# Gathered weights replaced by copies from a resident table in a two-layer conditional SSM kernel

## The chip, the cores and the metric

The kernel runs on one core of one Trainium2 chip. The metric is the device time of one execution in microseconds (us), from which smaller is better. Before the change the median of three runs is 1152.68 us (1152.45 to 1154.42). A "profile" here is one execution recorded by the hardware profiler; its engines are PE (TensorE matmul), PEld (TensorE weight load), DVE (VectorE), ACT (ScalarE), POOL (GpSimd) and SP (SyncE), the last of which only issues transfers.

## The reference

Two residual layers on `x` of shape (64 batches, 128 channels, 2048 steps), all float32.

```python
# layer 0: a batch chooses one of 16 weights of 128 x 128
W = weights[condition]                         # condition: 64 integers in 0..15
x = x + einsum('bct,bcd->bdt', x, W)
# layer 1: a diagonal state space model, 128 channels with 64 states each
K = 2 * einsum('hn,hnl->hl', Ct, exp(dtA * l)).real       # the kernel K(h, l) from log_dt, C, A
y = causal_convolution(x, K) + x * D[:, None]
x = x + y * (arange(2048) < length[batch])     # beyond a batch's length nothing is added
```

## The kernel before, in words

The sequence of 2048 is cut into two segments of 1024 (`SEGS`), and the work falls into two stages.

**Stage A, first segment of layer 0 and the tables of layer 1.** A loop over 64 batches calls `batch0(b)`. `fetch` brings two batches (1 MB) from HBM through SP's queue, nine pairs ahead (`AHEAD`). `weigh` brings the batch's weight with an indirect transfer on POOL's queue (L441), seven batches ahead (`WAHEAD`): the row numbers stand in the tile `rowid`, computed once by DVE. `add_one` (L449) adds the identity to it on DVE, four batches ahead (`ADD`), so that one matmul gives x + xW. `project` runs two matmuls of 128x512 (L457) into a PSUM tile of tag `y` (two buffers), ACT copies the result back over `xb` (L459), and ACT's queue writes it to the scratch `scr` in HBM (L462), from where stage B reads it in another layout.

Beside the batches runs the making of the tables. The setup (`_Parameters`, L116 on) computes rates, frequencies and gains on DVE in small instructions and lays them out by PE transposes (`lay`). From batch 12 on, every batch lets DVE take six steps of the generator `tables()`: for each of the 16 groups g (`NT`) `angles(g)` has 14 steps (L599 to L614) and `products(g)` two (L627, L629). `later(lag, step, g)` puts a group's other work so many batches on: `sines` on ACT (L623, L624) two batches after the angles, and, counted from the products, `lags` on PE one batch on (L641, eight small matmuls that give K), `keep_lags` on ACT two on (L645), `gain_lags` on DVE four on (L651), `store_lags` on POOL's queue six on (L655). `exps` on ACT (L487) come in fours of groups.

Each engine runs its instructions in the order in which this program writes them (the schedule is manual), so a waiting instruction holds everything behind it on its engine. In stage A PE's order is therefore batch, batch, eight `lags` matmuls, batch, and so on.

**Stage B, 64 iterations.** Each iteration handles four channels of one segment: `load` from `scr`, `turn` (PE transposes, L772), `inputs` (L797), `scan` over eight chunks on DVE (L812, L821), `inside` (L838), `outputs` (L850), then `copy_predicated` (L859), which puts the result over `xs` where `mask` is set, and `store`. While the first segment's 32 iterations run, `some(n)` works off the 128 projections ("pieces") of the second segment between the other matmuls; `fetches`, `weights_for` and `add_ones` bring their data, weights and identities ahead of them, by the iteration (`due`). POOL's queue also carries the Toeplitz tiles (L740), a memset (L782) and the carried states (L829).

Memory: the weight tiles `w1` have nine buffers (pool `s0`); the constants `ptab` (eight rows of parameters), `wk`, `drow`, `quarter`, `steps` and the integer `mask` lie in a pool that stays for the whole kernel.

Of the kernel before, what the change touches and what calls it, by code (L numbers as in the profile page):

```python
# [39 lines left out]
F32 = mybir.dt.float32  # L40
I32 = mybir.dt.int32
AF = mybir.ActivationFunctionType
ALU = mybir.AluOpType
# [3 lines left out]
P = 128  # L47
# [10 lines left out]

DRE, FHI, FLO, PHI, AMP, NAMPX, LR, LI = range(8)
NPAR = 8  # L60
Q = 128
SEGS = (1024, 1024)
TP = 4
# [49 lines left out]
class _Parameters:  # L113


    def __init__(self, nc, pool, psp, ptab, wk, ident, log_dt, c_in, log_a_real, a_imag):  # L116
        self.nc, self.V, self.psp, self.ptab, self.wk, self.ident = nc, nc.vector, psp, ptab, wk, ident
        N = self.N = a_imag.shape[1]
# [241 lines left out]

    def row(self, r0):
        return lambda lanes, f, n: self.ptab[lanes, r0 : r0 + n, :].rearrange("p k (j d) -> p k j d", d=2)

# [5 lines left out]
def cond_resid_ssm_kernel(  # L369
# [32 lines left out]
    assert C == P == Q and B == P // 2 and N == P // 2 and TP * Q == BK  # L402

    const = ctx.enter_context(tc.tile_pool(name="const", bufs=1))
    tab = ctx.enter_context(tc.tile_pool(name="tab", bufs=1))
    big = ctx.enter_context(tc.tile_pool(name="big", bufs=10))
    s0 = ctx.enter_context(tc.tile_pool(name="s0", bufs=9))
    dram = ctx.enter_context(tc.tile_pool(name="dram", bufs=1, space=DRAM))
# [6 lines left out]

    rowid = const.tile([P, B], I32, tag="rowid", name="rowid")
    ident = const.tile([P, P], F32, tag="ident", name="ident")
    ptab = const.tile([P, NPAR, NP], F32, tag="ptab", name="ptab")
    wk = const.tile([P, 2, NP, 2], F32, tag="wk", name="wk")
    drow = const.tile([2, NP], F32, tag="drow", name="drow")  # L420
    quarter = const.tile([P, 1], F32, tag="quarter", name="quarter")
    steps = const.tile([P, NE], F32, tag="steps", name="steps")
    mask = const.tile([P, NS, HL], I32, tag="mask", name="mask")

# [3 lines left out]
    AHEAD = 9  # L428
    WAHEAD = 7
    w_rows = weights.rearrange("s c d -> (s c) d")  # L430

# [6 lines left out]
    def weigh(s, b):  # L438

        w1s[s, b] = s0.tile([P, C], F32, tag="w1", name=f"w1_{s}_{b}")  # L440
        nc.gpsimd.indirect_dma_start(  # L441
            out=w1s[s, b],
            out_offset=None,
            in_=w_rows,
            in_offset=bass.IndirectOffsetOnAxis(ap=rowid[:, b : b + 1], axis=0),
        )

    def add_one(s, b):
        nc.vector.tensor_tensor(w1s[s, b], w1s[s, b], ident, ALU.add)  # L449

# [15 lines left out]

    ADD = 4
# [13 lines left out]
    def par_of(row, g, i):  # L481
        return ptab[:, row, g * TP + i : g * TP + i + 1]

    def exps(g):

        for i in range(TP):
            nc.scalar.activation(es[g][:, i, 0, :], steps, AF.Exp, scale=par_of(DRE, g, i))  # L487

    with tc.tile_pool(name="setup", bufs=1) as setup:
        ci = setup.tile([P, B], I32, tag="ci", name="ci")  # L490
        nc.sync.dma_start(ci, cond.rearrange("(o b) -> o b", o=1).to_broadcast([P, B]))
        par = _Parameters(nc, setup, psp, ptab, wk, ident, log_dt, c_in, log_a_real, a_imag)
        chi = setup.tile([P, 1], I32, tag="chi", name="chi")
        chf = setup.tile([P, 1], F32, tag="chf", name="chf")
        nc.gpsimd.iota(chi, [[0, 1]], base=0, channel_multiplier=1)
        make_identity(nc, ident)
# [3 lines left out]

        cf = setup.tile([P, B], F32, tag="cf", name="cf")
        ck = setup.tile([P, B], F32, tag="ck", name="ck")
        V.tensor_copy(chf, chi)
# [4 lines left out]
        V.tensor_copy(cf, ci)  # L508
# [3 lines left out]
        V.tensor_scalar(cf, cf, float(C), chf, ALU.mult, ALU.add)  # L512
        V.tensor_copy(rowid, cf)
        for b in range(WAHEAD):
# [42 lines left out]
        others = _weave(par.decays(), par.decay_of_chunk(), par.inverse())  # L557
        for b in range(ADD):
            run(_weave(freq, others), 8)
            add_one(0, b)  # L560
        run(freq)
# [6 lines left out]
        batch0(3)  # L568
        par.lay("ppar_1", rows, 3, par.row(DRE))
        run(par.gains())  # L570
# [8 lines left out]
        par.phase_sines()  # L579
        par.lay("ppar_2", rows, 1, par.row(PHI))  # L580
# [4 lines left out]
        par.lay("ppar_3", rows, 4, par.row(AMP), swapped=1)  # L585
        rows = par.spread("rows4", (par.wr, 1.0), (par.wi, 1.0))
# [39 lines left out]
    def products(g):  # L626
        V.tensor_tensor(es[g][:, :, 1, :], ts[g][:, 0], es[g][:, :, 0, :], ALU.mult)  # L627
        yield
        V.tensor_tensor(es[g][:, :, 0, :], ts[g][:, 1], es[g][:, :, 0, :], ALU.mult)  # L629
# [29 lines left out]
    FILL = 12  # L659
    begun = told = added = done = 0  # L660

# [23 lines left out]
    def add_ones(n):  # L685
        nonlocal added
        while added < min(n, len(pieces)):
            add_one(*pieces[added][:2])
            added += QB

# [28 lines left out]
    tmp.__exit__(None, None, None)  # L719


# [150 lines left out]
    def iteration(i):  # L872
# [6 lines left out]
        fetches(due(i + 1))  # L879
        weights_for(due(i + 2))  # L880
        if nxt:
# [17 lines left out]
        if nxt:  # L899
            inputs(i + 1, CG - 1)  # L900
            keep_weights(i + 1)
            add_ones(due(i + 1))
            scan(i + 1, 0, 2 if seg(i + 1)[0] == 0 else 1)
# [5 lines left out]
        if nxt:  # L909
            scan(i + 1, 3 if seg(i + 1)[0] == 0 else 2, NQ)  # L910
    add_ones(FILL)
    load(0)
# [37 lines left out]
```

## Time and profile before

| what | value |
|---|---|
| median of 3 runs | 1152.68 us |
| the profiled execution's own time | 1151.87 us |
| its span, first to last instruction | 1150.1 us |
| time outside the span | 1.77 us |
| mean granted TensorE clock | 0.991 of full |
| stage A (to the last projection of the first segment) | 0 to about 206 us |
| PE / DVE / ACT / POOL busy over the span | 94% / 75% / 60% / 26% |

The busy shares are means over two unlike stages and say little by themselves. What a change in a stage is worth is read from that stage: which engine works without a gap there, who waits for whom, and which chain of work ended last. An instruction's duration includes the overlap with the one before it; the time that it takes of its engine is better read from the starts of its neighbours.

### The profile page before, as it was taken

Reading aid. Unit: us, or ns where it says so; the run is one execution under the profiler, and the core shown is the slowest. Engines: PE = TensorE matmul, PEld = TensorE weight load, DVE = VectorE, ACT = ScalarE, POOL = GpSimd, SP = SyncE. Lnnn points to the kernel's source line nnn. Section 1 sums busy time; section 2 is a strip of 40 time slices with the busy share of each in tenths; the row PEclk is TensorE's granted clock in tenths of the full one; section 3 lists DMA queues with packets and bytes.
Section 4 is the critical chain, followed back from the end, with each engine's and each line's share of the span. In section 5 each row is a group of like instructions: output and inputs, shape, how many; then the busy total and the mean of one; then the engine's idle time right before and its main releaser. Section 6 shows DMA issues by size and latency. Waiting matters only on the chain.

```text
span 1150.1 us, 23651 instructions
## 1 busy us (share of the span) xinstructions
PE 1081.0 (94%) x8586; PEld 792.1 (69%) x8586; DVE 867.6 (75%) x2940; ACT 694.0 (60%) x1117; POOL 296.6 (26%) x377
## 2 busy tenths in 40 slices
PE   4587889799999999999999999999999999999996
PEld 2233344367767777777777777888888888888885
DVE  7498895076667667766766677889899899889896
ACT  2557875566666566566656666656656656656551
POOL 5233444322331332233223211221111111111110
PEclk9899999999999999999999999999999999999998
DMA  8999999989999999999999978788887787788854
GB/s 324 411 399 352 386 355 336 365 288 312 308 329 297 310 299 293 317 309 293 298 308 299 291 227 231 228 237 228 216 238 226 217 242 222 212 242 222 212 162 110
DMA packets 120501, 320.62 MB, mean 279 GB/s; under 512 B 13602, under 2 KB 13858, under 8 KB 112194
## 3 DMA queue, kind: packets, MB, share of 16 engines
q1 hardware_dynamic: 70800, 218.16, 61.7%
q10 hardware_dynamic: 35762, 67.32, 15.8%
q0 software_dynamic: 13824, 33.65, 10.6%
q8 instruction: 68, 1.11, 0.4%
q14 instruction: 47, 0.39, 0.1%
HBM read 172.13 MB, written 146.93 MB: 277 GB/s over the span
## 4 chain that ended last, share of the span: by engine, by line
PE 81%; DVE 6%; ACT 5%; DMA 5%; issue 1%; ACTq 1%; SPq 0%; DVEq 0%
PE y L850 21%; PE y L838 19%; PE v L797 18%; PE p L457 11%; PE tr L772 10%; DMA xb<-in_x_dram 2%; PE pb L754 2%; ACT xb L459 1%; DMA scr<-xb 1%; ACT e L487 1%; PE pk L641 1%; DMA x<-scr 1%; DVE t L606 1%; DMA aim<-in_L_cond_A_imag_dram 1%; DVE s L812 1%
## 5 line engine op out<-in xcount | busy, mean ns | idle before, releaser
L812 DVE SCALAR_TENSOR_TENSOR s<-s,ptab 128x128 f32<-128x128 f32 x1792 | 525.7, 355 | 83.3 <-ACT s L802 77.3
L802 ACT ACTIVATE s<-v,ptab 64x512 f32<-64x512 f32 (+1 forms) x512 | 336.7, 658 | 49.8 <-PE v L797 34.2
L838 PEld LDWEIGHTS y<-tt,u 128*128 128x128 f32 x2048 | 263.5, 192 | 80.6 <-issue 67.0
L457 PE MATMUL p<-xb,w 128*128 128x512 f32 x512 | 254.2, 612 | 35.8 <-ACT xb L459 20.7
L838 PE MATMUL y<-tt,u 128*128 128x128 f32 x2048 | 269.9, 275 | 0.2 <-DVE x L859 0.2
L850 PEld LDWEIGHTS y<-e,s 64*128 64x128 f32 x4096 | 233.9, 188 | 46.5 <-issue 24.2
L797 PE MATMUL v<-u,bt 128*128 128x512 f32 (+1 forms) x512 | 248.4, 567 | 0.0
L850 PE MATMUL y<-e,s 64*128 64x128 f32 x4096 | 246.7, 275 | 1.4 <-DVE s L812 1.4
L773 ACT COPY u<-tr 128x512 f32<-128x512 f32 x256 | 150.8, 589 | 157.9 <-PE tr L772 132.3
L821 DVE TENSOR_SCALAR s<-s 128x128 f32<-128x128 f32 x448 | 106.6, 238 | 136.8 <-ACT s L802 136.8
L459 ACT COPY xb<-p 128x512 f32<-128x512 f32 (+1 forms) x192 | 139.3, 726 | 110.8 <-PE p L457 94.3
L859 DVE COPY_PREDICATED x<-mask,y 128x1024 f32<-128x1024 int32 x128 | 171.2, 1338 | 1.1 <-PE y L850 1.0
L441 POOL DMA_INDIRECT w<-in_L_cond_weights_dram,rowid x128 | 131.3, 1026 | 120.0 <-PE p L457 70.5
L457 PEld LDWEIGHTS p<-xb,w 128*128 128x128 f32 x512 | 87.3, 195 | 108.6 <-issue 47.6
L772 PE MATMUL tr<-ident,x 128*128 128x128 f32 x1024 | 156.3, 275 | 5.5 <-DMA x<-scr 5.5
L772 PEld LDWEIGHTS tr<-ident,x 128*128 128x128 f32 x1024 | 121.8, 142 | 56.5 <-issue 51.0
L829 POOL DMA_DIRECT2D carry<-s x64 | 45.1, 755 | 256.5 <-DVE w L449 215.1
L740 POOL DMA_DIRECT2D tt<-kpad x64 | 51.3, 802 | 182.2 <-DVE s L812 171.4
L797 PEld LDWEIGHTS v<-u,bt 128*128 128x128 f32 x512 | 79.6, 191 | 13.9 <-issue 13.6
L785 POOL DMA_DIRECT2D s<-carry x64 | 45.0, 708 | 130.5 <-PE y L850 119.1
L755 ACT COPY bt<-pb 128x512 f32<-128x512 f32 x32 | 18.8, 587 | 87.2 <-PE pb L754 86.6
L782 POOL MEMSET s<- 128x384 f32 x32 | 13.6, 424 | 117.6 <-DMA carry<-s 46.7
(171 smaller groups left out, 357.3 us busy)
## 6 DMA issues: line engine op xcount, KB each, us to landing
xb<-in_x_dram SPq DMA_DIRECT2D x64, 1024.0 KB, 10.9
scr<-xb ACTq DMA_DIRECT2D x128, 512.0 KB, 8.4
x<-scr SPq DMA_DIRECT2D x64, 1024.0 KB, 8.4
out_dram<-x SPq DMA_DIRECT2D x128, 512.0 KB, 5.9
tt<-kpad POOLq DMA_DIRECT2D x64, 256.0 KB, 6.5
btd<-bt SPq DMA_DIRECT2D x32, 256.0 KB, 8.3
bt<-btd SPq DMA_DIRECT2D x32, 256.0 KB, 4.9
carry<-s POOLq DMA_DIRECT2D x64, 64.0 KB, 7.6
```

Source lines behind the costliest of these rows:

```text
L441: nc.gpsimd.indirect_dma_start(out=w1s[s, b], out_offset=None, in_=w_rows, in_offset=bass.IndirectOffsetOnAxis(ap=rowid[:, b : b + 1], axi ...
L457: nc.tensor.matmul(ps[:, k], w1s[s, b], own[:, cols], start=True, stop=True)
L459: nc.scalar.copy(own[:, cols], ps.rearrange("p k t -> p (k t)"))
L772: nc.tensor.transpose(tr[:, k, :], xs[i][:, c, k * Q : (k + 1) * Q], ident)
L773: nc.scalar.copy(u, tr)
L797: nc.tensor.matmul(v[:, 0:nv], w, us[i, n].rearrange("p k r -> p (k r)")[:, 0:nv], start=True, stop=True)
L802: nc.scalar.activation(own[:, 0:nv], v[lanes, 0:nv], AF.Copy, scale=amp)
L812: nc.vector.scalar_tensor_tensor(new[:, d, 0:2], src, factor, own[:, d, 0:2], ALU.mult, ALU.add)
L821: nc.vector.tensor_scalar(old[:, :, 2], old[:, :, 0], -1.0, None, ALU.mult)
L838: nc.tensor.matmul(y[:, k, :], u[:, k, :], tts[i][:, n, :], start=(k == 0), stop=False, skip_group_check=True)
L850: nc.tensor.matmul(ys[i, d][:, c, k, :], st[half[c], d, part, k, :, :].rearrange("p f b -> p (f b)"), e[half[c], pair % TP, part, 0:Q], st ...
L859: nc.vector.copy_predicated(xs[i][:, d::2, :].rearrange("r c (k t) -> r c k t", k=KK), keep_k.unsqueeze(1).to_broadcast([P, 2, KK, Q]), ys ...
```

## The change

The 16 weights (1 MB) are brought once into the tile `wres` by one plain transfer, the first on SP's queue, and DVE adds the identity to all 16 in one instruction of 128x2048 elements. A batch's weight is then copied by POOL from `wres` into a `w1` tile: POOL loads the batch's condition from SBUF into a register and uses it as the offset of the copy. The indirect transfers, `rowid`, and the per-batch `add_one` go. `w1` has four buffers instead of nine and `weigh` runs three batches ahead; for the second segment it is called from `some`, piece by piece, instead of once per iteration.

The matmuls for K and what follows them move two batches on: `lags`, `keep_lags`, `gain_lags`, `store_lags` stand 3, 4, 6 and 8 batches after the products (before: 1, 2, 4, 6), and the loop has two more rounds.

The mask is stored in bytes instead of 32-bit integers. The tables needed only in stage A (`gtab`, the first four rows of the former `ptab`, and `wk`, `drow`, `quarter`, `steps`) move to a pool `early` that is released before stage B. The conditions are read as one row by ACT's queue, ahead of the parameters.

```diff
-    s0 = ctx.enter_context(tc.tile_pool(name="s0", bufs=9))
+    s0 = ctx.enter_context(tc.tile_pool(name="s0", bufs=4))
-    rowid = const.tile([P, B], I32, tag="rowid", name="rowid")
+    ci = const.tile([1, B], I32, tag="ci", name="ci")
+    wres = const.tile([P, S, C], F32, tag="wres", name="wres")
-    mask = const.tile([P, NS, HL], I32, tag="mask", name="mask")
+    mask = const.tile([P, NS, HL], I8, tag="mask", name="mask")
-    WAHEAD = 7
+    WAHEAD = 3
     def weigh(s, b):
         w1s[s, b] = s0.tile([P, C], F32, tag="w1", name=f"w1_{s}_{b}")
-        nc.gpsimd.indirect_dma_start(out=w1s[s, b], out_offset=None, in_=w_rows,
-            in_offset=bass.IndirectOffsetOnAxis(ap=rowid[:, b : b + 1], axis=0))
-    def add_one(s, b):
-        nc.vector.tensor_tensor(w1s[s, b], w1s[s, b], ident, ALU.add)
+        at = nc.values_load(ci[:, b : b + 1], engines=(mybir.EngineType.Pool,), min_val=0, max_val=S - 1, ...)
+        nc.gpsimd.tensor_copy(w1s[s, b], wres[:, bass.ds(at, 1), :].rearrange("p s d -> p (s d)"))
     def batch0(b):
...
-        if b + ADD < B:
-            add_one(0, b + ADD)
...
-        nc.sync.dma_start(ci, cond.rearrange("(o b) -> o b", o=1).to_broadcast([P, B]))
+        nc.scalar.dma_start(craw, cond.rearrange("(o b) -> o b", o=1))
+        nc.sync.dma_start(wres, weights.rearrange("s c d -> c s d"))
...
-        V.tensor_copy(rowid, cf)
+        V.tensor_copy(ci, cf)
+        V.tensor_tensor(wres, wres, ident.unsqueeze(1).to_broadcast([P, S, C]), ALU.add)
...
-        for lag, step in ((1, lags), (2, keep_lags), (4, gain_lags), (6, store_lags)):
+        for lag, step in ((3, lags), (4, keep_lags), (6, gain_lags), (8, store_lags)):
...
         for s, b, q in pieces[done : done + n]:
+            weights_for(done + WAHEAD * QB + 1)
             project(s, b, q, ...)
-    def add_ones(n): ...                      # and its calls
-            weights_for(FILL)                 # at batch 60
-        weights_for(due(i + 2))               # in iteration(i)
-    for now in range(12, B + 7):
+    for now in range(12, B + 9):
     tmp.__exit__(None, None, None)
+    early.__exit__(None, None, None)
```

More of the change, by code (lines that the diff above doesn't have):

```diff
@@ L56 @@
 LOG2E = 1.0 / math.log(2.0)
-DRE, FHI, FLO, PHI, AMP, NAMPX, LR, LI = range(8)
-NPAR = 8
+DRE, FHI, FLO, PHI = range(4)
+AMP, NAMPX, LR, LI = range(4)
+NPAR = 4
 Q = 128
@@ L113, with __init__ @@
 class _Parameters:
-    def __init__(self, nc, pool, psp, ptab, wk, ident, log_dt, c_in, log_a_real, a_imag):
-        self.nc, self.V, self.psp, self.ptab, self.wk, self.ident = nc, nc.vector, psp, ptab, wk, ident
+    def __init__(self, nc, pool, psp, wk, ident, log_dt, c_in, log_a_real, a_imag):
+        self.nc, self.V, self.psp, self.wk, self.ident = nc, nc.vector, psp, wk, ident
         N = self.N = a_imag.shape[1]
@@ L359, in lay, with row @@
                 self.V.tensor_copy(to(lanes, f, n)[:, swapped], got[:, 1 - f, swapped])
-    def row(self, r0):
-        return lambda lanes, f, n: self.ptab[lanes, r0 : r0 + n, :].rearrange("p k (j d) -> p k j d", d=2)
+    def row(self, table, r0):
+        return lambda lanes, f, n: table[lanes, r0 : r0 + n, :].rearrange("p k (j d) -> p k j d", d=2)
     def weight(self, lanes, f, n):
@@ L402, in cond_resid_ssm_kernel @@
     assert C == P == Q and B == P // 2 and N == P // 2 and TP * Q == BK
+    I8 = mybir.dt.uint8
     const = ctx.enter_context(tc.tile_pool(name="const", bufs=1))
@@ L414, in cond_resid_ssm_kernel @@
     carry = dram.tile([NP, P, 2, B], F32, tag="carry", name="carry")
-    rowid = const.tile([P, B], I32, tag="rowid", name="rowid")
+    ci = const.tile([1, B], I32, tag="ci", name="ci")
+    wres = const.tile([P, S, C], F32, tag="wres", name="wres")
     ident = const.tile([P, P], F32, tag="ident", name="ident")
     ptab = const.tile([P, NPAR, NP], F32, tag="ptab", name="ptab")
[L419 to L422, printed above, removed]
-    mask = const.tile([P, NS, HL], I32, tag="mask", name="mask")
+    mask = const.tile([P, NS, HL], I8, tag="mask", name="mask")
     xbs, w1s = {}, {}
@@ L428, in cond_resid_ssm_kernel @@
     AHEAD = 9
-    WAHEAD = 7
-    w_rows = weights.rearrange("s c d -> (s c) d")
+    WAHEAD = 3
     def fetch(s, n):
@@ L440, in weigh @@
         w1s[s, b] = s0.tile([P, C], F32, tag="w1", name=f"w1_{s}_{b}")
[L441 to L445, printed above, removed]
-        )
-    def add_one(s, b):
-        nc.vector.tensor_tensor(w1s[s, b], w1s[s, b], ident, ALU.add)
+        at = nc.values_load(
+            ci[:, b : b + 1],
+            engines=(mybir.EngineType.Pool,),
+            min_val=0,
+            max_val=S - 1,
+            skip_runtime_bounds_check_because="it is clamped above",
+        )
+        nc.gpsimd.tensor_copy(w1s[s, b], wres[:, bass.ds(at, 1), :].rearrange("p s d -> p (s d)"))
     def project(s, b, q, ps, n_banks=1):
@@ L465, in project @@
                 del xbs[s, n]
-    ADD = 4
     def batch0(b):
@@ L481, in par_of @@
     def par_of(row, g, i):
-        return ptab[:, row, g * TP + i : g * TP + i + 1]
+        return gtab[:, row, g * TP + i : g * TP + i + 1]
     def exps(g):
@@ L487, in exps @@
             nc.scalar.activation(es[g][:, i, 0, :], steps, AF.Exp, scale=par_of(DRE, g, i))
-    with tc.tile_pool(name="setup", bufs=1) as setup:
-        ci = setup.tile([P, B], I32, tag="ci", name="ci")
-        nc.sync.dma_start(ci, cond.rearrange("(o b) -> o b", o=1).to_broadcast([P, B]))
[L492 to L495, printed above, removed]
+    early = tc.tile_pool(name="early", bufs=1)
+    earlies = early.__enter__()
+    gtab = earlies.tile([P, NPAR, NP], F32, tag="gtab", name="gtab")
+    wk = earlies.tile([P, 2, NP, 2], F32, tag="wk", name="wk")
+    drow = earlies.tile([2, NP], F32, tag="drow", name="drow")
+    quarter = earlies.tile([P, 1], F32, tag="quarter", name="quarter")
+    steps = earlies.tile([P, NE], F32, tag="steps", name="steps")
+    with tc.tile_pool(name="setup", bufs=1) as setup:
+        craw = setup.tile([1, B], I32, tag="craw", name="craw")
+        nc.scalar.dma_start(craw, cond.rearrange("(o b) -> o b", o=1))
+        nc.sync.dma_start(wres, weights.rearrange("s c d -> c s d"))
+        par = _Parameters(nc, setup, psp, wk, ident, log_dt, c_in, log_a_real, a_imag)
         make_identity(nc, ident)
@@ L498, in cond_resid_ssm_kernel @@
             fetch(0, n)
-        cf = setup.tile([P, B], F32, tag="cf", name="cf")
-        ck = setup.tile([P, B], F32, tag="ck", name="ck")
-        V.tensor_copy(chf, chi)
+        cf = setup.tile([1, B], F32, tag="cf", name="cf")
+        ck = setup.tile([1, B], F32, tag="ck", name="ck")
         V.memset(quarter, math.pi / 2)
@@ L507, in cond_resid_ssm_kernel @@
         V.memset(zero, 0.0)
-        V.tensor_copy(cf, ci)
+        V.tensor_copy(cf, craw)
         V.tensor_scalar(ck, cf, 0.0, float(S), ALU.is_lt, ALU.mult)
@@ L511, in cond_resid_ssm_kernel @@
         V.tensor_scalar(cf, cf, 0.0, float(S - 1), ALU.max, ALU.min)
-        V.tensor_scalar(cf, cf, float(C), chf, ALU.mult, ALU.add)
-        V.tensor_copy(rowid, cf)
+        V.tensor_copy(ci, cf)
+        V.tensor_tensor(wres, wres, ident.unsqueeze(1).to_broadcast([P, S, C]), ALU.add)
         for b in range(WAHEAD):
@@ L557, in cond_resid_ssm_kernel @@
         others = _weave(par.decays(), par.decay_of_chunk(), par.inverse())
-        for b in range(ADD):
-            run(_weave(freq, others), 8)
-            add_one(0, b)
+        run(_weave(freq, others), 32)
         run(freq)
@@ L568, in cond_resid_ssm_kernel @@
         batch0(3)
-        par.lay("ppar_1", rows, 3, par.row(DRE))
+        par.lay("ppar_1", rows, 3, par.row(gtab, DRE))
         run(par.gains())
@@ L579, in cond_resid_ssm_kernel @@
         par.phase_sines()
-        par.lay("ppar_2", rows, 1, par.row(PHI))
+        par.lay("ppar_2", rows, 1, par.row(gtab, PHI))
         run(par.sizes())
@@ L584, in cond_resid_ssm_kernel @@
         batch0(11)
-        par.lay("ppar_3", rows, 4, par.row(AMP), swapped=1)
+        par.lay("ppar_3", rows, 4, par.row(ptab, AMP), swapped=1)
         rows = par.spread("rows4", (par.wr, 1.0), (par.wi, 1.0))
@@ L659, in cond_resid_ssm_kernel @@
     FILL = 12
-    begun = told = added = done = 0
+    begun = told = done = 0
     def due(i):
@@ L683, in weights_for @@
             told += QB
[L685 to L689, printed above, removed]
     plan = {}
@@ L901, in iteration @@
             keep_weights(i + 1)
-            add_ones(due(i + 1))
             scan(i + 1, 0, 2 if seg(i + 1)[0] == 0 else 1)
@@ L910, in iteration @@
             scan(i + 1, 3 if seg(i + 1)[0] == 0 else 2, NQ)
-    add_ones(FILL)
     load(0)
```

## The prediction

> **What bounds the kernel now.** I read the page's slices first (one bound or several?), then busy time by stretch, then who idles in stage A and for whom, then one handover in order of time.
>
> ```profile
> span 1150.1 us, 23651 instructions
> ...
> PE   4587889799999999999999999999999999999996
> ...
> DVE  7498895076667667766766677889899899889896
> ...
> DMA  8999999989999999999999978788887787788854
> ...
> PE 81%; DVE 6%; ACT 5%; DMA 5%; issue 1%; ACTq 1%; SPq 0%; DVEq 0%
> ```
>
> In the view of stretches the columns are length, then busy time (count) of PE, PEld, DVE, ACT and POOL, granted clock, DMA share, GB/s:
>
> ```profile
> 56.60:183.80 127.20, 104.31 (x379) 47.09 (x378) 114.83 (x307) 89.07 (x140) 53.04 (x55) 0.99 1.01 375
> 183.80:206.00 22.20, 22.16 (x86) 10.95 (x87) 5.93 (x20) 11.23 (x14) 10.32 (x13) 1.00 0.85 311
> 231.60:700.00 468.40, 467.50 (x3709) 342.95 (x3708) 321.32 (x1100) 295.52 (x483) 126.29 (x164) 1.00 0.95 298
> 700.00:1127.00 427.00, 427.00 (x4150) 359.82 (x4150) 377.40 (x1287) 260.27 (x422) 77.16 (x108) 1.00 0.79 220
> ```
>
> From 231.6 to 1127 us PE works without a gap and the chain lies on it; DVE, ACT and POOL have room. What the change does there is worth nothing unless it makes PE wait. All that can move is in the first 206 us, mostly in the 127.2 us (43 batches, 2.96 each) where tables and batches run together and no engine is full. The waits of DVE, PE and ACT in that stretch (total us, times, longest):
>
> ```profile
> DVE krow L651 <- ACT krow L645: 8.6, 6, 2.5
> ...
> PE p L457 <- ACT xb L459: 11.2, 12, 1.8
> PE pk L641 <- DVE e L629: 9.9, 10, 1.9
> ...
> ACT xb L459 <- PE p L457: 20.9, 11, 6.3
> ```
>
> the row of the adds in the same stretch (busy us, mean ns, idle before):
>
> ```profile
> L449 DVE TENSOR_TENSOR w<-w,ident 128x128 f32<-128x128 f32 x43 | 12.2, 285 | 0.0
> ```
>
> and one handover:
>
> ```profile
> 83.08 0.70 DVE L629 TENSOR_TENSOR e<-t,e 128x516 f32<-128x516 f32 x1
> 83.69 0.28 DVE L449 TENSOR_TENSOR w<-w,ident 128x128 f32<-128x128 f32 x1
> 83.83 1.92 PE L641 MATMUL pk<-e,wk 128*2 128x128 f32 x16 [1.86 <-DVE e L629]
> 83.89 0.87 DVE L599 TENSOR_SCALAR t<-steps,ptab 128x129 f32<-128x129 f32 x4
> 87.69 1.01 ACT L459 COPY xb<-p 128x1024 f32<-128x1024 f32 x1 [2.58 <-PE p L457]
> ```
>
> PE idles 1.86 us for DVE's product, then does the K matmuls, and ACT, behind both, idles 2.58. The chain of this stretch changes hands so four times: DVE until 83.8, PE and ACT until 104, DVE until 118, PE and ACT until 139, DVE, PE and ACT from 144, DVE from 169 to 183.8, then PE to 205.5. So four resources take turns. Their needs in the 127.2 us, waits left out:
> - DVE 127.2 - 8.6 (krow) = 118.6;
> - ACT 89.1 busy + 43 scr issues of 0.37 and their gaps of 0.04 = 106.7;
> - PE 104.3;
> - DMA: the stretch 56 to 183 moves 47.6 MB, and where the DMA is pressed (the opening) it holds about 405 GB/s: 117.6.
>
> The stretch is 1.07 times the largest need. That factor is the price of taking turns, and I use it again.
>
> **The change part by part.**
>
> *Weights no longer gathered.* From 56 to 183 GpSimd's queue moves 2.74 MB (43 gathers, a few tiny kpad writes). DMA's need falls to 44.9/0.405 = 110.8 us.
>
> *No add per batch.* 43 adds leave DVE. Each lasts 0.285 but takes 0.20 of the engine (83.69 to 83.89): -8.6 us, at most 12.2. DVE's need becomes 110.0. No transfer stands in front of DVE any more.
>
> *GpSimd's copy, 128x128.* No row shows it. Nearest rows: GpSimd's memset of 128x128 took 0.197 us, its select of 128x128 0.294, against 1.044 for a gather's issue, so POOL itself gains. But GpSimd can hold up DVE:
>
> ```profile
> 15.66 0.57 POOL L529 IOTA ti<- 128x512 int32 x1
> 15.73 0.59 DVE L181 TENSOR_SCALAR tk<-turns 128x128 f32<-128x128 f32 x1
> ```
>
> The same DVE shape took 0.221 us elsewhere (L171); here it ended only after the iota. So a copy may cost DVE nothing or as much as that stretch, 0.37: 0 to +15.9 us on 43. Gathers disturb DVE too (L150, 0.44 against about 0.2, beside one), and that leaves, so below nothing is possible: -0.2 x 43 = -8.6 at the other end. A copy of 0.2 to 0.3 beside a DVE that works nine tenths of the time, half of it met, is 0.13; minus half of that for the gathers' own, I take +0.07, that is +3 us. DVE's need: 113.
>
> The Trainium skill, "SBUF — State Buffer", section "Who interferes with whom", speaks against the change: GpSimd and DVE share one port pair as an exclusive lock, and a DVE instruction with two SBUF inputs collides with a GpSimd instruction that reads SBUF, though not with one that only writes. The rows agree for the iota and the one-input instruction; a copy, which reads, would by that page also hold L603, L608, L612 and the products. By it each of 43 copies costs DVE its 0.29 us, and the sum below would end 10 us later.
>
> *The register load before each copy.* No row shows one. The ends: GpSimd's gap before an issue, 0.3 us, and a whole gather's way to landing, median 6.0. I take 1 us, near the sequencer-side rows (0.3 to 1.0), since it fetches one word. Load and copy, 1.3 us, lie beside PE's 2.96 per batch, and the copy stands three batches ahead of its matmul. Without that cover PE would wait: the third rival. The kpad store, the only other thing on POOL's queue here, waits for DVE's gain; it is two batches behind that gain and five ahead of the batch whose weight queues behind it.
>
> The Trainium skill, "DMA: Bandwidth & Descriptors", section "Latency and other measured facts", gives a register load a floor of about 600 ns. By that the pair would be 0.9 us and the sum would not change.
>
> *K matmuls two batches on.* PE's 9.9 us of waits for products go, and with them a part of ACT's 20.9. The PE count stays. krow, gain and store keep their distances, so DVE's krow wait stays possible and is what comes next: a quicker DVE meets ACT (106.7) sooner. For 56.6 to 183.8: largest need 113 (DVE), times 1.07 = 121: **-6 us**. Bounds: no turn-taking left, 111, -16; the lock in full on top, 110 + 15.9 = 126 x 1.07 = 135, +8.
>
> *From 183.8 to 206* PE is full with nine batches of 1.75 and three K groups of 1.85, left because PE stood one batch behind DVE. Two batches on, at most two of them (3.5 us) are done earlier; ACT's pace hinders that, so half: **-1.7 us**.
>
> *Opening, to 56.6 us.* The new 1 MB stands first on SP's queue ahead of nine fetches, and the add of 128x2048 delays DVE's chain. By 516 elements in 0.70 us, 2048 are 2.8; with the wait for the 1 MB DVE's setup starts 2 to 5 us later than 7.4. That is hidden: DVE idles for more than half of 30 to 56 us (busy 11.0 of 26.0), where the DMA at 410 GB/s sets the pace. There 1.05 MB come and 1.38 MB of GpSimd's queue leave: -0.8 us; the first batch's data come up to 2.6 us later (1.05 MB at 410). **0**, bounds -1 and +3.
>
> *Handover, 206 to 231.6.* The chain lies on scr's write and the 8.9 us load of x; ten gathers (0.65 MB at 371 GB/s, 1.8 us) no longer share it: **-0.5**, bounds 0 and -1.8. The first four copies of the second segment wait for slots of the last batches, inside that gap of 5.5 us on PE. The first Toeplitz tile is issued behind seven copies, some 5 us later than now (208.4), and is first read at 231.6, so it is covered.
>
> *Stage B.* 13.9 us of adds leave DVE and 60 copies come to POOL, both beside a full PE. POOL's carry, Toeplitz and memset wait up to 3 us longer behind copies; each has over 10 us before its reader. `copy_predicated` with a byte mask: no row; 1.34 now, of which three lie in the closing chain. As nothing is known, 0, bounds -1 and +1. Bound by engine it would need 50% more, since DVE is 88% busy. **0**.
>
> Sum on the profiled execution: 1151.87 (span 1150.1 and 1.77 around it) - 6 - 1.7 + 0 - 0.5 = 1143.7. The median is 0.8 above that execution: **1144.5 us**.
>
> **The rivals.**
>
> 1. *The gain goes into GpSimd's hold on DVE or into ACT.* For: DVE does 92 instructions of 0.7 us that a copy may meet; ACT's 106.7 is close to the rest. Against: the 128x128 rows of GpSimd are short. Stretch 56.6 to 183.8 at -2 to +2, the rest as summed: 1148.5 to 1152.5, say 1150.5.
>
> 2. *Turn-taking vanishes.* For: PE's ten waits for products are what couples the two halves. Against: ACT still waits for DVE's angles and DVE for ACT's krow, two batches apart. Stretch at 111 (-16), closing -3.5, handover -1: 1152.7 - 20.5 = 1132; half-way 1137, which I take.
>
> 3. *Slower: the register load makes POOL the pace.* Place: batches 12 to 63. It decides once load and copy exceed 2.96 us, or 1.75 in the last nine batches. At 3.5 us: 52 x 0.54 = +28, 1180; where it only passes 1.75 by 1 us, in the last nine batches and the second segment's first four, less three ahead: +10, with the gains lost 1162. At the far end, 6.3 us a batch, 52 x 3.3 = +172. Against: POOL now issues 1.04 us gathers and idles 74 us of the stretch. The first rival's lock at its full bound (+8 instead of -6) gives 1158.5 and is counted here.
>
> 4. *The change does nothing for the end:* PE's stage B hides it. Excluded, since stage B starts with a load that waits for stage A's last scr write.
>
> **How the numbers follow.** Forecast (1141 to 1148.5) 0.52; first rival 0.17; second 0.15; third 0.16. What differs from 1152.7 by less than 0.2% (2.3 us) can't be told from no change. Faster: 0.52 + 0.15 + a little of the first = 0.70; same, the rest of the first: 0.13; slower 0.17. The range leaves out the far half of the second rival (below 1136) and most of the third (above 1155): 1136 to 1155. The forecast's own is 1141 to 1148.5.
>
> **What would show it.** L449 gone and DVE from 57 us to its last product in 118 to 122 us; PE's K matmuls waiting under 2 us for L629; the last first-segment batch at 197 to 200 us instead of 206; stage B's rows unchanged. Wrong if L603 to L629 lengthen beyond 0.8 us (lock), if `p` waits for POOL (register load), if DVE's krow wait grows past 12 us (ACT), or if the first batches start more than 3 us late.

## The result, and the profile after

The changed kernel takes 1138.1 us (median of 4; 1137.11 to 1140.83) against 1153.37 us for the kernel before (median of 4). The medians differ by 15.3 us; the ratio estimated from the single runs is 0.9875, 95% interval 0.9863 to 0.9888, that is 14.4 us less (12.9 to 15.8). The forecast was 1144.5 us, 1136 to 1155. Sign and range held, but the gain is nearly twice the 8.2 us of the sum, it lies outside the forecast's own 1141 to 1148.5, and it does not lie where the sum put it.

The profiled execution after took 1140.83 us, the longest of its four, and that of before (1151.87) was among the shorter of its kernel. So the two traces show only 11.0 us of the 14.4, and 1 to 3 us of scatter must be allowed wherever a step is read from one trace below.

The page's head, PE's slices and the chain after:

```profile
span 1139.1 us, 23806 instructions
...
PE   5598889899999999999999999999999999999996
...
PE 88%; DMA 5%; ACT 4%; DVE 1%; issue 1%; ACTq 0%; POOLq 0%; POOL 0%; SPq 0%; DVEq 0%
```

DVE's share of the chain falls from 6% to 1%, PE's rises from 81% to 88%. To see where the 11.0 us went, both traces are cut at the same four events: the start of ACT's copy of batch 12, of batch 58 and of batch 63 (the last of the first segment), and the first matmul of `outputs`. The view of stretches (columns as in the prediction), before:

```profile
58.96:196.94 137.98, 115.05 (x441) 53.12 (x440) 116.72 (x311) 94.29 (x147) 56.59 (x60) 1.00 1.00 370
196.94:205.52 8.58, 8.58 (x21) 3.80 (x20) 1.75 (x7) 5.53 (x6) 6.53 (x8) 1.00 0.79 277
205.52:244.64 39.12, 31.77 (x120) 16.58 (x119) 9.82 (x40) 25.25 (x41) 9.13 (x12) 0.96 0.97 379
```

and after, with the two long stretches of stage B:

```profile
56.25:190.27 134.02, 117.52 (x425) 53.79 (x425) 110.21 (x262) 93.64 (x146) 26.18 (x58) 0.96 0.99 362
190.27:200.90 10.63, 10.63 (x37) 4.93 (x36) 0.31 (x2) 6.00 (x8) 3.61 (x9) 1.00 0.61 227
200.90:234.12 33.22, 30.24 (x121) 15.67 (x119) 8.87 (x36) 25.09 (x41) 6.86 (x16) 1.00 1.00 379
...
221.10:689.50 468.40, 467.46 (x3709) 342.93 (x3708) 308.85 (x1045) 294.83 (x484) 97.28 (x166) 1.00 0.94 296
689.50:1116.50 427.00, 427.00 (x4150) 359.81 (x4150) 374.67 (x1286) 259.37 (x422) 76.87 (x108) 1.00 0.77 220
```

Differences: opening -2.7, batches 12 to 58 -4.0, batches 58 to 63 +2.1 (one K group more falls behind batch 58), handover -5.9, all behind it -0.5. Sum: -11.0. In this trace the clock granted to PE in batches 12 to 58 is 0.96, before the change 1.00; more on that in the last section. Stage B is the same to 0.1 us in its rows. More than half of the gain lies in the opening and the handover, which the sum priced at 0 and -0.5.

The waits after, in batches 12 to 58 (total us, times, longest):

```profile
POOL w L446 <- PE p L454: 112.9, 46, 10.8
...
ACT xb L456 <- PE p L454: 25.0, 14, 6.3
DVE krow L647 <- ACT krow L641: 12.5, 6, 3.4
PE p L454 <- ACT xb L456: 9.5, 6, 2.5
...
PEld pk L637 <- DVE e L623: 4.6, 6, 0.8
...
PE p L454 <- POOL w L446: 2.7, 2, 1.4
```

PE's matmuls for K no longer wait for products at all; only weight loads do, 4.6 us in pieces of at most 0.8. GpSimd waits 112.9 us for PE to free weight tiles, so it is ahead of its work. Two waits of PE (2.7 us) and four of its weight loads (9.1 us) are put down to a copy nonetheless. PE's two end at 89.45 and 166.37; the copies of GpSimd ended at 88.57 and 165.42, ACT's copies of `xb` at 89.35 and 166.27. PE starts 0.1 us behind ACT's copy both times, so by the times it waited for that, and the name of the releaser is wrong.

### The profile page after: what moved, and what is told of

Same layout as the page of the kernel before. It is cut to its first block, busy times and chain, and to the rows that moved or that the text cites. A ratio compares the mean times of both kernels' runs of the same rounds, so it can differ in the third digit from the quotient of the medians.

```text
span 1139.1 us, 23806 instructions
## 1 busy us (share of the span) xinstructions
PE 1084.4 (95%) x8586; PEld 793.4 (70%) x8586; DVE 842.5 (74%) x2811; ACT 692.1 (61%) x1117; POOL 215.4 (19%) x376
## 3 DMA queue, kind: packets, MB, share of 16 engines
q10 hardware_dynamic: 35764, 67.32, 15.8%
## 4 chain that ended last, share of the span: by engine, by line
PE 88%; DMA 5%; ACT 4%; DVE 1%; issue 1%; ACTq 0%; POOLq 0%; POOL 0%; SPq 0%; DVEq 0%
PE y L841 21%; PE y L829 20%; PE v L788 18%; PE p L454 16%; PE tr L763 10%; DMA xb<-in_x_dram 3%; PE pk L637 2%; PE pb L745 2%; ACT xb L456 1%; DMA scr<-xb 1%; ACT e L480 1%; DVE s L803 1%; DMA x<-scr 0%; ACTq L459 0%; ACT L480 0%
## 5 line engine op out<-in xcount | busy, mean ns | idle before, releaser
L803 DVE SCALAR_TENSOR_TENSOR s<-s,ptab 128x128 f32<-128x128 f32 x1792 | 520.4, 344 | 98.1 <-ACT s L793 80.0
L454 PE MATMUL p<-xb,w 128*128 128x512 f32 x512 | 259.4, 624 | 37.1 <-ACT xb L456 15.7
L812 DVE TENSOR_SCALAR s<-s 128x128 f32<-128x128 f32 x448 | 98.9, 221 | 137.3 <-ACT s L793 137.3
L850 DVE COPY_PREDICATED x<-mask,y 128x1024 f32<-128x1024 uint8 x128 | 166.7, 1302 | 1.1 <-PE y L841 1.0
L446 POOL COPY w<-wres 128x128 f32 x128 | 53.9, 421 | 330.1 <-PE p L454 308.0
L776 POOL DMA_DIRECT2D s<-carry x64 | 44.9, 706 | 128.3 <-PE y L841 114.4
```

The source lines that it names most:

```text
L446: nc.gpsimd.tensor_copy(w1s[s, b], wres[:, bass.ds(at, 1), :].rearrange("p s d -> p (s d)"))
L454: nc.tensor.matmul(ps[:, k], w1s[s, b], own[:, cols], start=True, stop=True)
L803: nc.vector.scalar_tensor_tensor(new[:, d, 0:2], src, factor, own[:, d, 0:2], ALU.mult, ALU.add)
L812: nc.vector.tensor_scalar(old[:, :, 2], old[:, :, 0], -1.0, None, ALU.mult)
L850: nc.vector.copy_predicated(xs[i][:, d::2, :].rearrange("r c (k t) -> r c k t", k=KK), keep_k.unsqueeze(1).to_broadcast([P, 2, KK, Q]), ys ...
```

## The experiments

The theory taken to the chip: several resources hold stage A in turn, so the gain is a sum of parts (the shift of the K matmuls, the gathers' share of the DMA, a lighter handover), with the additions on DVE worth little by themselves. Rivals: the shift is all, the DMA is all, DVE's additions are all. "Before" below is the kernel before timed with those runs; its median was 1153.0 to 1153.7 us. e1 to e4, e5 to e8 and e9 to e12 ran on three chips. The ratios are estimated from the single runs and are not the quotients of the medians.

| kernel | median us | ratio to before, 95% interval |
|---|---|---|
| changed kernel | 1138.10 | 0.9875 (0.9863 to 0.9888) |
| changed kernel again (e5) | 1139.01 | 0.9872 (0.9857 to 0.9887) |
| ... short distances (e1) | 1143.05 | 0.9908 (0.9891 to 0.9925) |
| ... transfers put back (e2) | 1142.94 | 0.9906 (0.9887 to 0.9926) |
| ... additions put back (e3) | 1140.00 | 0.9880 (0.9863 to 0.9897) |
| ... transfers in the handover (e4) | 1141.64 | 0.9902 (0.9881 to 0.9923) |
| ... e1, e2 and e3 together (e8) | 1148.50 | 0.9956 (0.9943 to 0.9969) |
| ... first Toeplitz tile early (e9) | 1145.85 | 0.9929 (0.9915 to 0.9944) |
| ... distances 2, 3, 5, 7 and copies seven ahead (e12) | 1141.12 | 0.9890 (0.9866 to 0.9913) |
| before, with long distances (e6) | 1151.82 | 0.9988 (0.9977 to 0.9999) |
| before, no gathers for the second segment (e7) | 1148.78 | 0.9961 (0.9948 to 0.9974) |
| before, no additions in the first segment (e10) | 1151.00 | 0.9982 (0.9972 to 0.9991) |
| before, first Toeplitz tile late (e11) | 1150.78 | 0.9981 (0.9972 to 0.9990) |

**Control.** The changed kernel unedited.

> The changed kernel itself once more, beside the other runs of this chip, as the control for differences of 1 to 4 us. By every theory 1138 to 1139.5, and its 64th copy of a batch at 198 to 201 us.

1139.01 us (1138.15 to 1140.51); the copies of batches 12, 58 and 63 start at 55.96, 189.96 and 200.58. Differences from it below are read against this scatter. Single stretches scatter more: e4 and e9 (below) are the changed kernel unedited up to batch 58, and there the four traces have 134.0 us (after), 134.0 (e5), 131.1 (e4) and 131.9 (e9) for batches 12 to 58, and start batch 12 between 55.96 and 56.83. Traces of kernels that are the kernel before up to there (e7, e11) have 137.8 and 137.9.

**The shift alone, both ways.** e1 puts the short distances back, e6 gives the long ones to the kernel before:

```diff
-        for lag, step in ((3, lags), (4, keep_lags), (6, gain_lags), (8, store_lags)):
+        for lag, step in ((1, lags), (2, keep_lags), (4, gain_lags), (6, store_lags)):
-    for now in range(12, B + 9):
+    for now in range(12, B + 7):
```

> The changed kernel with lags, keep_lags, gain_lags and store_lags back at 1, 2, 4 and 6 batches; everything else stays as changed. My theory: the first 206 us are held by several resources in turn, and the gain (15.3 us on the medians, 11.0 in the profiled spans) is DMA and DVE relief in the stretch and the opening (about 7), a lighter handover (about 4) and the uncoupling of PE from DVE's products (about 3). Then this kernel is 2 to 4 us above the changed kernel, 1140 to 1142, and PE's K matmuls wait again for L623, some 5 to 10 us in all. Rival 'the shift of the K matmuls is the whole gain of the stretch': 8 us or more above the changed kernel (1146 or more). Rival 'the shift is for nothing, because DVE without its adds is early enough': within 1 us of the changed kernel.

> The kernel before with only the shift: lags, keep_lags, gain_lags and store_lags at 3, 4, 6 and 8 batches, two more rounds of the loop; gathers and additions as they were. Going back to the short distances cost the changed kernel 4 us. If the shift is a part of its own, it takes 3 to 5 us off before (1148 to 1150), with batches 12 to 58 at about 134 us instead of 138. If the shift pays only where DVE's additions are gone: less than 1 us. If it is what opens the whole gain of the stretch: 6 or more.

e1 costs 4.0 us against the control, a little more than expected. Batches 12 to 58 take 138.5 us instead of 134.0, batches 58 to 63 8.8 instead of 10.6. Of PE's waits there, in e1:

```profile
PE pk L637 <- DVE e L625: 6.5, 5, 1.9
PE p L454 <- ACT xb L456: 6.1, 5, 1.9
```

and in e6, where this is PE's only one:

```profile
PE p L457 <- ACT xb L459: 16.7, 12, 2.4
```

PE's matmuls wait for products again in e1 (6.5 us) and no longer in e6. In e6 batches 12 to 58 go from 138.0 to 132.3 us although gathers and additions are all there; 2.0 of these 5.7 us come back in batches 58 to 63, and its handover takes 40.8 instead of 39.1, so the whole kernel gains only 1.4 us (0.1 to 2.7), less than the 3 to 5 expected. The shift is a part of its own, the largest in the stretch, and worth 1 to 4 us at the end.

**DVE's additions, both ways.** e3 adds an unused addition per batch to the changed kernel; e10 leaves the additions of the first segment out of the kernel before.

```diff
+        if b >= 12:
+            extra = earlies.tile([P, C], F32, tag="extra", name=f"extra_{b}", bufs=4)
+            nc.vector.tensor_tensor(extra, wres[:, 0, :], ident, ALU.add)
         project(0, b, 0, psp.tile([P, QB, BK], F32, tag="y", name=f"p0_0_{b}", bufs=2), QB)
```

```diff
     def add_one(s, b):
-        nc.vector.tensor_tensor(w1s[s, b], w1s[s, b], ident, ALU.add)
+        if s == 1:
+            nc.vector.tensor_tensor(w1s[s, b], w1s[s, b], ident, ALU.add)
```

> The changed kernel with one DVE addition of 128x128 into an unused tile in each of the batches 12 to 63 (52 additions, as the additions of the identity were; nothing reads them). My theory, that DVE's need shows only where DVE holds PE, which is rare after the change: 52 x 0.20 = 10.4 us of DVE, of which 1 to 3 us show. Rival 'DVE was the bound of the stretch, as the prediction's sum has it': +8 to +10 us. Rival 'DVE is covered': within 0.7 us.

> The kernel before without the 64 additions of the identity on DVE for the first segment (left out there: the plus x of layer 0); gathers and distances as before. The prediction's sum takes 8.6 us of DVE out of the stretch and makes 6 us of it, two of them through the DMA. If DVE's need was the bound while PE stood one batch behind it: 5 to 9 us faster than before, batches 12 to 58 in 129 to 133 us. My theory now, that PE's place behind DVE's products and the DMA set the stretch: 1 to 3 us. If additions cost nothing at all: within 0.7 us.

e3: +1.0 us, not told from nothing by its interval, and seen in its trace ahead of batch 12 (57.13 instead of 55.96), where no additions were put; batches 12 to 58 take 134.2 us, the changed kernel's 131.1 to 134.0. e10, which leaves out the plus x of the first segment's layer 0: -2.1 us (1.0 to 3.2); batches 12 to 58 take 135.5 instead of 138.0. So the additions cost some 2 us while PE stands one batch behind the products, and nothing that these runs can tell from scatter once it stands three behind. How much of the 2 us lies in the stretch is less sure: e1 has neither additions nor gathers there, and takes 138.5. What e10 still has is PE's wait for products:

```profile
PE p L458 <- ACT xb L460: 11.7, 11, 2.1
PE pk L642 <- DVE e L630: 7.5, 6, 1.8
```

**The transfers of the first segment.**

```diff
         nc.gpsimd.tensor_copy(w1s[s, b], wres[:, bass.ds(at, 1), :].rearrange("p s d -> p (s d)"))
+        if s == 0:
+            extra = earlies.tile([P, C], F32, tag="extra", name=f"extra_{b}", bufs=4)
+            nc.gpsimd.dma_start(extra, weights[b % S])
```

> The changed kernel, in which GpSimd's queue brings a 64 KB weight from HBM into an unused tile beside each of the 64 copies for the first segment (4 MB in all, as the gathers did; nothing reads it). My theory, that the DMA's need is one of the terms: 10 us (4.2 MB at 405 GB/s) of transfers, of which a third to a half shows: +3 to +5 us over the changed kernel. Rival 'DMA traffic is the whole gain': +9 to +13, that is the time of before. Rival 'DMA traffic is hidden': within 1 us.

+3.9 us, within what was expected, but not where: batch 12 starts at 58.79 instead of 55.96, batches 12 to 58 take 134.2. The transfers cost 2.8 us in the opening, more than its scatter; the 0.2 of the stretch is within the scatter there, so a cost of up to 3 us in it is not excluded. The opening's DMA from 9 us to the copy of batch 12, before:

```profile
DMA packets 7145, 19.86 MB, mean 397 GB/s; under 512 B 792, under 2 KB 920, under 8 KB 7142
```

and after:

```profile
DMA packets 6572, 18.84 MB, mean 399 GB/s; under 512 B 500, under 2 KB 628, under 8 KB 6569
```

Same rate, 1.02 MB less: 2.6 us. GpSimd's queue moved 1.38 MB of that before and nothing after, ACT's 0.14 MB less; SP's moves 0.50 MB more. The first 9 us move the same amount in both kernels (1.88 and 1.87 MB).

**All three together.** The edits of e1, e2 and e3 in one kernel.

> The changed kernel with the three things put back at once: distances 1, 2, 4, 6, a 64 KB transfer beside each copy of the first segment, and an unused DVE addition of 128x128 in each of the batches 12 to 63. Alone they cost about 4, 4 and 1 us. If they add up, 1147 to 1148.5, and the rest to 1153.4 is the handover's. If the same waits are counted twice (DMA and shift take each other's place): 1144 to 1146. If DVE's additions matter once PE stands one batch behind DVE: 1150 or more.

1148.5 us, 9.5 above the control; alone they cost 4.0, 3.9 and 1.0, in sum 8.9. Within the scatter they add up. What remains to before, some 5 us, fits what they do not touch: the handover, whose 33.4 us in e8 are the changed kernel's 33.2, against 39.1 before.

**The handover.** Before, in order of time (SPq and POOL issue transfers, PE consumes):

```profile
208.42 0.83 POOL L740 DMA_DIRECT2D tt<-kpad  x1
210.33 2.06 SPq L733 DMA_DIRECT2D x<-scr  x3
...
219.32 1.09 PE L772 MATMUL tr<-ident,x 128*128 128x128 f32 x4 [5.54 <-DMA x<-scr]
220.21 1.92 PE L457 MATMUL p<-xb,w 128*128 128x512 f32 x2
```

and after:

```profile
204.98 1.60 SPq L724 DMA_DIRECT2D x<-scr  x3
...
208.09 0.78 POOL L731 DMA_DIRECT2D tt<-kpad  x1 [0.81 <-issue]
...
210.29 0.63 PE L763 MATMUL tr<-ident,x 128*128 128x128 f32 x4 [1.04 <-DMA x<-scr]
210.76 1.06 PE L454 MATMUL p<-xb,w 128*128 128x512 f32 x2
```

From its issue to the first transpose the load takes 9.0 us before and 5.3 after. Two things left its neighbourhood: the gathers, and the first Toeplitz tile (256 KB), which stood 1.9 us ahead of the load and now stands 3.1 us behind it. And the first matmuls after the gap are quicker: two of 128x512 take 1.06 us instead of 1.92. Four kernels take this apart. e4 puts ten 64 KB transfers into the changed kernel; e7 takes the second segment's gathers out of before and leaves out the choice of the weight there:

```diff
+        if now in (60, B + 6):
+            for b in range(6 if now == 60 else 4):
+                extra = earlies.tile([P, C], F32, tag="extra", name=f"extra_{now}_{b}", bufs=10)
+                nc.gpsimd.dma_start(extra, weights[b])
```

```diff
         w1s[s, b] = s0.tile([P, C], F32, tag="w1", name=f"w1_{s}_{b}")
+        if s == 1:
+            nc.gpsimd.tensor_copy(w1s[s, b], ident)
+            return
         nc.gpsimd.indirect_dma_start(
```

e9 moves the tile ahead of the load in the changed kernel, e11 behind it in the kernel before:

```diff
     load(0)
     load(1)
-    some(8)
+    some(3)
+    toeplitz(0)
+    some(5)
...
         if nxt:
-            toeplitz(i + 1)
+            if i >= 0:
+                toeplitz(i + 1)
```

```diff
         if nxt:
-            toeplitz(i + 1)
+            if i == 0:
+                toeplitz(0)
+            if i >= 0:
+                toeplitz(i + 1)
```

> The changed kernel with ten 64 KB transfers from HBM into unused tiles on GpSimd's queue, six after batch 60 and four after the last round of the loop, where before ten gathers lay before and in the handover. If these gathers are what made the handover slow (its load of 1 MB took 8.9 us, after the change 5.2): +3 to +5 us over the changed kernel, and the first load takes 7 us or more again. If the load's time comes from something else, for example from when it meets the transfers for the second segment: 0 to +1 us; by the prediction's own sum +0.5.

> The kernel before, in which the weights of the second segment are not gathered: GpSimd copies the identity into the tile instead, so no 64 KB transfers lie in the handover and in stage B (left out: the choice of the weight for the second segment). If the twelve gathers between 194 and 212 us are what stretches the first load (8.9 us against 5.2) and the steps after it, the time from the 64th copy of a batch to the first output matmul falls from 39.1 us to 33 to 35, and the kernel is 4 to 6 us faster than before. By the prediction's own price for the handover, 0.5 us. If something else stretches it (the Toeplitz tile's transfer, the second segment's x): 0 to 1 us.

> The changed kernel, in which the first Toeplitz tile's transfer is issued on GpSimd's queue after five of the second segment's weight copies instead of after seven, that is at about 203 us, some 2 us ahead of the load of the first 1 MB of stage B, as it stood before the change (208.42 against 210.33; in the changed kernel 208.09 against 204.98). Theory 'the order of these two transfers is the other half of the handover': the load's way to the first transpose grows from 5.2 to 7 or 8 us, and the kernel is 1.5 to 3 us slower than the changed kernel. Rival 'only the gathers stretch the handover': 5.2 to 5.6 us, within 0.7 us of the changed kernel.

> The kernel before, in which the first Toeplitz tile's transfer is issued one iteration later, just before the second one, at about 212.5 us and so behind the load of the first 1 MB (210.3) instead of ahead of it; everything else as before, the gathers too. Theory 'order of the transfers': the load's way to the first transpose falls from 9.0 to 6.5 to 7.5 us and the kernel is 1.5 to 2.5 us faster than before. Rival 'only the gathers': 8.5 to 9 us, within 0.7 us of before.

| kernel | load's issue to first transpose | last copy (batch 63) to first transpose | first transpose to first output matmul | PE's wait for the load |
|---|---|---|---|---|
| after | 5.3 | 9.4 | 23.8 | 1.0 |
| e4 | 6.0 | 11.2 | 24.8 | 2.3 |
| e11 | 7.0 | 11.8 | 25.4 | 3.5 |
| e7 | 7.4 | 11.6 | 26.3 | 3.3 |
| e9 | 8.1 | 12.2 | 26.4 | 3.8 |
| before | 9.0 | 13.8 | 25.3 | 5.5 |

The load is 1.6 us shorter without the gathers (e7) and 2.0 shorter with the tile behind it (e11); together that is 3.6 of the difference of 3.7. Putting the tile ahead in the changed kernel (e9) brings 2.8 back. Both expectations "only the gathers" and "0.5" fall. A part of the second column lies ahead of the load's issue: from the last copy to it 4.8 us before, 4.2 in e7, 4.1 after, so the gathers delay it too, by 0.6 us. On the whole, e11 gains 2.2 us (1.2 to 3.2), as expected. e9 loses 6.8 against the control, more than expected: in the traces 2.9 to the first transpose, 2.4 to the first output, and 1.6 behind it, less 1.2 ahead of the handover. The 1.6 lie at the very end: the last forty matmuls take 4.13 us at a granted clock of 0.66 in 1130 to 1135 us, in the control 2.50 at full clock. No trace shows whether the other executions of e9 have that too. e7 gains 4.5 us (3.0 to 6.0) as expected, but its last copy and its first output lie 37.9 us apart and not 33 to 35, only 1.2 less than before; PE has half clock longer there than before (`v` at 220.36 us takes 1.92 us, before at 222.61 only 1.02), and the rest of its gain stays open. e4 costs 2.6 us, less than the 3 to 5 expected, and its load takes 6.0 us and not 7; its interval reaches that of the control. It also does not put the transfers back where they stood: it issues them at 189.5 to 198 us, 5 us and more ahead of the load (203.03), while before four of the gathers were issued at 205.8 to 211.7, around the load (210.33). So e4 says little against the gathers' 1.6 us.

The last column goes with the rest. In these handovers the clock granted to PE is lower behind the longer waits. e9's first matmuls:

```profile
211.50 1.09 PE L763 MATMUL tr<-ident,x 128*128 128x128 f32 x4 [3.81 <-DMA x<-scr]
212.38 1.92 PE L454 MATMUL p<-xb,w 128*128 128x512 f32 x2
```

and the stretch view of e9 beside it (clock third from the end):

```profile
210.00:215.00 5.00, 3.50 (x11) 2.36 (x12) 0.00 (x0) 1.17 (x2) 0.00 (x0) 0.50 1.00 415
215.00:220.00 5.00, 5.00 (x14) 2.02 (x13) 0.00 (x0) 3.19 (x6) 1.48 (x3) 0.82 1.02 415
```

At half clock the same matmuls take nearly twice their time, here until about 217 us. Before, 220 to 225 us ran at 0.76; after, the whole handover ran at 1.00. From the first transpose to the first output the kernels with a late load need 1.5 to 2.5 us more than after (third column). Not all of that has to be the clock: e4 needs 1.0 more at full clock.

**An attempt at a quicker kernel.**

```diff
-        for lag, step in ((3, lags), (4, keep_lags), (6, gain_lags), (8, store_lags)):
+        for lag, step in ((2, lags), (3, keep_lags), (5, gain_lags), (7, store_lags)):
-    for now in range(12, B + 9):
+    for now in range(12, B + 8):
-        if b + WAHEAD < B:
-            weigh(0, b + WAHEAD)
+        if b + 7 < B:
+            weigh(0, b + 7)
-        for b in range(WAHEAD):
+        for b in range(7):
```

with the first segment's weight tiles in nine buffers of `early`.

> An attempt at a quicker kernel: the changed kernel with distances 2, 3, 5 and 7 (one batch less than the change made them) and the copies of the first segment's weights seven batches ahead in nine buffers, which lie in the memory released before stage B. If one batch of distance is enough to uncouple PE from DVE's products, one K group less is left for the last nine batches (1.85 us); if PE's waits for GpSimd's copies (2.7 us named, more behind its own sequencer) are real, they go too: 1135.5 to 1138. If distance 2 couples PE to DVE again: 1140 to 1142, as with distance 1 (1143). If neither matters: 1138.5 to 1139.5.

1141.12 us, 1136.79 to 1144.94: no gain, and too wide to tell from the changed kernel. The time lies in the range for "if distance 2 couples PE to DVE again", but no matmul of PE waits for products in its trace. Its copies of batches 12, 58 and 63 start at 56.71, 190.70 and 201.11, as the changed kernel's within 0.5 us. The waits of PE put down to GpSimd's copies stay too (2.3 us in batches 12 to 58, after the change 2.7), though the copies now stand seven batches ahead. They too end 0.1 us after a copy of `xb` by ACT: the longest at 90.31, ACT's copy at 90.21, GpSimd's at 89.70.

## Why the prediction was right in sign and half right in size

By its number the result is nearer to the second rival (1137) than to the forecast, but that rival's terms did not come either: in full it had -16 for the stretch and -3.5 for the closing, and 1137 stands for the way to it half done; measured were -4.0 and +2.1. That the range held is in part luck, since the misses below have both signs: the stretch and the closing gave less than the sum has, the opening and the handover more.

- *"For 56.6 to 183.8: largest need 113 (DVE), times 1.07 = 121: -6 us."* The size is near (-4.0 for batches 12 to 58), the mechanism is wrong. The sum took DVE's need as the measure and priced the shift only through it. DVE's busy time fell by 6.5 us, from 116.7 to 110.2, yet its way from the first table instruction to its fourteenth last-step product (the one that ends at 183.8 before; two more follow) fell only from 127.2 to 124.2 us, not to 118 to 122. e3 and e10 put the additions at 0 to 2.5 us, e1 and e6 the shift at 4.5 to 5.7 in this stretch, each from single traces in which the changed kernel's own stretch scatters by 3. Needs times a factor was not how this stretch worked; the one wait named in the prediction, PE behind `e`, was.
- *"DMA's need falls to 44.9/0.405 = 110.8 us"*: nothing seen of it in this stretch (e2, 0.2 us, within the scatter); what the transfers cost is seen in the opening.
- *"From 183.8 to 206 ... -1.7 us."* No such gain. PE is as full there as before, and batches 58 to 63 take 2.1 us more, since one K group more falls behind batch 58. The last first-segment batch is copied at 200.9, just outside 197 to 200.
- *Opening: "0, bounds -1 and +3."* Measured -2.7, outside the bounds. The working let 1.05 MB come against 1.38 that leave, and then took the rest away again for a late start of the first batches. The gathers' 1.38 MB left as it said, but of some 1.05 MB of other data on SP's queue that the weights push out of the first 9 us only 0.50 come back before the copy of batch 12; the rest falls behind it. That DVE's start 3.5 us later (10.85 instead of 7.38) is hidden was right: its first table instruction came at 53.45 instead of 56.56.
- *Handover: "ten gathers (0.65 MB at 371 GB/s, 1.8 us) no longer share it: -0.5, bounds 0 and -1.8."* Measured -5.9. The gathers' 1.8 was right in size (e7, 1.6 on the load and 0.6 ahead of its issue), though only four of the ten are issued after 205.7 us; cutting it to 0.5 was not. Two terms were missing: the Toeplitz tile, which the working did place *"some 5 us later than now"* but looked at only for its reader and not for the load that it leaves alone (2.0, e11), and PE's clock after its wait, visible in the trace of before as 1.09 us for four transposes that take 0.63 elsewhere (at most 1.5 us).
- *The register load, "I take 1 us"; load and copy 1.3 us.* Too much. The first copies after the addition stand back to back:

```profile
8.64 2.29 DVE L511 TENSOR_TENSOR wres<-wres,ident 128x2048 f32<-128x2048 f32 x1 [5.55 <-DMA wres<-in_L_cond_weights_dram]
...
10.99 0.29 POOL L446 COPY w<-wres 128x128 f32 x1 [9.68 <-DVE wres L511]
...
11.46 0.29 POOL L446 COPY w<-wres 128x128 f32 x1 [0.18 <-issue]
```

  The pair takes 0.47 us, and the loads alone 0.28 to 1.24, in the median 0.29. The third rival never came near its point of 2.96, as the 112.9 us of GpSimd's waits for PE say. By the Trainium skill, "DMA: Bandwidth & Descriptors", section "Latency and other measured facts", the load alone has a floor of about 600 ns; here the median load takes half of that, so the measurement decides.
- *GpSimd's hold on DVE, "+0.07 each".* Not seen on DVE. Its instructions with two inputs after:

```profile
L604 DVE TENSOR_TENSOR t<-t 128x516 f32<-128x516 f32 x16 | 11.3, 704 | 0.5
L599 DVE TENSOR_TENSOR t<-t 128x516 f32<-128x516 f32 x15 | 10.6, 704 | 0.5
```

  Before, the same two took 700 and 696 ns. It is the copy that pays: 0.29 us alone in the opening, 0.42 in the mean over the kernel, and GpSimd has that time. Why it is longer was not tested. The lock that the Trainium skill's "SBUF — State Buffer", section "Who interferes with whom", describes, which the prediction weighed, is consistent with this only with GpSimd as the loser; its +10 us did not come.
- *DVE's krow wait "is what comes next"*: it grew from 10.4 to 12.5 us between batches 12 and 58, and from 8.6 to 9.2 in the prediction's own window of 56.6 to 183.8, so its sign of 12 us did not come. Partly right; ACT's `xb` behind PE's `p` stayed at 25.
- *Stage B, 0, byte mask 0 (+-1)*: right; `copy_predicated` takes 1302 instead of 1338 ns.

## What to carry to other kernels

Where several resources take turns, price each wait in the chain that the change removes, not the need of the busiest engine: here moving the consumer two batches away did more in the stretch (4.5 to 5.7 us) than taking 43 instructions off the producer (0 to 2.5), though each alone on the kernel before gains about the same (1.4 and 2.1 us). Look at what a change moves on every queue near a handover, and ask which large transfer the late one now meets or misses; a tile that is "covered" can still be in the way of a load that isn't. And read the matmuls right behind a gap of PE: if they run at nearly twice their usual length, the gap costs more than itself.

## What the runs showed of the hardware

In the handovers PE's granted clock fell to about half after waits for a load of 3.3, 3.8, 5.5 and 7.3 us (e7, e9, before, e6: the first four transposes took 1.09 us), partly after 3.5 (e11: 0.76), and not after 1.0 or 2.3 (after, e4: 0.63). The Trainium skill, "TensorE: Matmul & The Clock Gate", section "HAM oscillation — how this bites in real kernels", gives 3.4 us as the longest idle gap; these rows agree roughly. In batches 12 to 58 no such length holds. The changed kernel's own trace:

```profile
122.93 3.45 PE L454 MATMUL p<-xb,w 128*128 128x512 f32 x4 [2.53 <-ACT xb L456]
126.68 1.96 PE L454 MATMUL p<-xb,w 128*128 128x512 f32 x4 [0.30 <-issue]
...
132.37 5.37 PE L454 MATMUL p<-xb,w 128*128 128x512 f32 x8 [1.89 <-ACT xb L456]
```

with the clock at 0.57 from 122 to 126 us and 0.73 from 134 to 138, and the same places in e4, the same kernel up to there, at full clock:

```profile
121.54 1.96 PE L454 MATMUL p<-xb,w 128*128 128x512 f32 x4 [1.10 <-ACT xb L456]
125.29 1.96 PE L454 MATMUL p<-xb,w 128*128 128x512 f32 x4 [1.79 <-issue]
...
130.98 3.67 PE L454 MATMUL p<-xb,w 128*128 128x512 f32 x8 [1.89 <-ACT xb L456]
```

The last wait is 1.89 us in both, and only one has a lower clock behind it; the control (e5) has e4's waits of 1.8 and 1.89 us and 5.37 us behind them. So the length of one wait does not decide it here, and what does is open. Between the first and the last row the changed kernel falls behind e4 by 3.1 us: 1.4 from the ACT copy that PE waits for at 122.93, and 1.7 from the eight matmuls at 132.37. The slow ones at 122.93 cost nothing, since the wait behind them is shorter by as much. With granted clocks of 0.96, 0.97, 0.98 and 0.99 the stretch takes 134.0 (after), 134.0 (e5), 131.1 (e4) and 131.9 us (e9), while before has 1.00. So a part of what the change gains there can be lost again to the clock, as much as the scatter of these kernels' times. That this is the scatter's cause was not shown; it is seen in four traces.
